# A selective scan behind a deformable convolution: delta*u*B made by ScalarE and TensorE in two one-bank PSUM tiles, one state at a time

## The chip, the cores and the metric

The kernel runs on one core of a Trainium2 chip. Its engines are TensorE (PE, with its weight loads as PEld), VectorE (DVE), ScalarE (ACT), GpSimd (POOL) and SyncE (SP, which issues most DMAs). Each works through its own queue in order, and semaphores hold an instruction until what it needs is there. The metric is the device time of one execution in microseconds; less is better.

## The reference, cut to what matters

Two layers, each `x = x + layer(group_norm(x))`, on x of 4 images x 128 x 128 x 128 channels, float32. The first is a deformable convolution in two groups (offsets, bilinear samples gathered from the image, a depthwise and a pointwise convolution). The second is two Mamba blocks, for which every image row of 128 pixels is a sequence of its own. The change lies in the scan of such a block:

```python
xz = h @ in_w
u, res = jnp.split(xz, 2, axis=-1)
u = silu(causal_conv4(u))                      # 256 channels
dt, Bm, Cm = jnp.split(u @ xw, [8, 24], axis=-1)   # 16 states
delta = softplus(dt @ dtw + dtb)
A = -jnp.exp(A_log)
# per sequence, channel d and state n, over time t:
#   h[t] = exp(delta[t,d] * A[d,n]) * h[t-1] + delta[t,d] * u[t,d] * Bm[t,n]
#   y[t,d] = sum over n of h[t] * Cm[t,n]
y = y + u * Dp
return y * silu(res) @ ow
```

## The kernel before

**First layer.** `layer0(b)` walks image b in 32 x 9 = 288 units. For each unit `gather` issues eight indirect DMAs on GpSimd (line 364), which fetch the bilinear neighbours of 128 pixels each into `gt`. `sample` multiplies them by their weights on VectorE (`gw`, line 382), adds the four neighbours by accumulating transposes on TensorE into one PSUM bank `p4` (in the profile `p`; the helper `add_transposed`, line 128), and ScalarE copies that bank out (`s`, line 396). `add_up` then adds nine taps into the accumulators `acc` (line 415), some 60 matmul instructions for each of five units in nine.

**Second layer.** A job is four image rows (512 time steps, four sequences) of one Mamba block; there are 128 x 2 = 256 jobs. `pre` prepares a job: `u`, `g`, the projection `dbl` that holds dt, B and C, then `delta` (tile `de`) and `du` = delta*u, both with channels on the partitions, in NC = 2 chunks of 128 channels. `pre` of the next job is emitted ahead of `main` of this one. `main` takes the 16 states in eight steps of NQ = 2 states. In each step:

- SP broadcasts two rows of B and two of C over all partitions from DRAM (`bc`, 512 KB each, line 570);
- ScalarE computes the decays exp(delta*A) into one of three tiles `da` that all steps share (line 580); the first element of each sequence is set to zero (line 575), which starts the recurrence anew, so that one scan can run over all of chunks, states and sequences;
- VectorE multiplies du by B into `hs` (line 584), scans `da` in place with `hs` (line 591, 2048 elements a partition) and multiplies by C (line 595);
- TensorE adds the result over states by 16 accumulating transposes into `y` in PSUM, two banks (line 128).

After the last step `g = y * silu(res)` is formed (line 606), transposed back (`pyg`, `yg`) and projected (`pout`).

**Order.** The end of the program emits the units of the next image's first layer among the steps of this image's second layer, so that the first layer of image b+1 ends three jobs before the second layer of image b. The first layer of image 0 runs alone at the start, the second layer of image 3 alone at the end. The order within each engine's queue is then set when the program is built, by a scheduler that follows the emitted order as a priority; nothing is reordered while it runs.

**PSUM.** [...] pool `ps` (first layer, two), `psa` (`acc`, two), `ps1` (preparation and projection, two), `psy` (`y`, two).

Of the kernel before, what the change touches and what calls it, by code (L numbers as in the profile page):

```python
# [10 lines left out]
F32 = mybir.dt.float32  # L11
# [6 lines left out]
P = 128  # L18
# [45 lines left out]
def block_kernel(ctx: ExitStack, tc: tile.TileContext, a: dict, out: bass.AP):  # L64
# [27 lines left out]
    ps = ctx.enter_context(tc.tile_pool(name="l0ps", bufs=2, space=PSUM))  # L92
# [3 lines left out]
    ps1 = ctx.enter_context(tc.tile_pool(name="l1ps", bufs=2, space=PSUM))  # L96
# [29 lines left out]
    def add_transposed(o, v, start, stop):  # L126

        nc.tensor.matmul(o, v, ident, is_transpose=True, start=start, stop=stop, skip_group_check=True)  # L128
# [34 lines left out]
    cvw = loadw("cvw", [P, NL, DCONV, NC * P], pool=p2, tag="hs")  # L163
    for l in range(NL):
        nc.vector.tensor_tensor(
            inc[:, l], cvw[:, l], inw[:, l].unsqueeze(1).to_broadcast([P, DCONV, NC * P]), ALU.mult
        )
# [295 lines left out]
    das = [cw.tile([P, NC, NQ, SR, P], F32, name=f"da{i}") for i in range(NDA)]  # L463
    zero = cw.tile([P, NC * NQ * SR], F32, name="zero")
    nc.vector.memset(zero, 0.0)
# [18 lines left out]
    def pre(st, l):  # L484
# [40 lines left out]
        bcd = pd.tile([2 * NS, TB], F32, tag="bcd", name=f"bcd_{nm}")  # L525
        nc.sync.dma_start(bcd, dbl[DTR + 1 : XP, :])
# [3 lines left out]
        du = p2.tile([P, NC, TB], F32, tag="du", name=f"du_{nm}", bufs=2)  # L530
# [20 lines left out]
        st.update(u=u, g=g, delta=de, du=du, bcd=bcd)  # L551

    def main(st, l):
# [11 lines left out]
        for q in range(NS // NQ):  # L565
            bc = []
            for w in range(2):
                t = p2.tile([P, NQ, TB], F32, tag=f"bc{w}", name=f"bc{w}_{nm}_{q}", bufs=2)
                n0 = w * NS + q * NQ
                nc.sync.dma_start(t, st["bcd"][n0 : n0 + NQ, :].partition_broadcast(P))  # L570
                bc.append(t)
            da = das[n_da[0] % NDA]
            n_da[0] += 1

            nc.scalar.copy(da.rearrange("p c n s t -> p (c n s) t")[:, :, 0], zero)
            for c in range(NC):
                dv = st["delta"][:, c].rearrange("p (s t) -> p s t", s=SR)
                for n in range(NQ):
                    s = q * NQ + n
                    nc.scalar.activation(  # L580
                        da[:, c, n, :, 1:], dv[:, :, 1:], AF.Exp, scale=aneg[:, l, c, s : s + 1]
                    )
            hs = p2.tile([P, NC, NQ, TB], F32, tag="hs", name=f"hs_{nm}_{q}")
            nc.vector.tensor_tensor(  # L584
                hs,
                st["du"].unsqueeze(2).to_broadcast([P, NC, NQ, TB]),
                bc[0].unsqueeze(1).to_broadcast([P, NC, NQ, TB]),
                ALU.mult,
            )
            df = da.rearrange("p c n s t -> p (c n s t)")  # L590
            nc.vector.tensor_tensor_scan(  # L591
                df, df, hs.rearrange("p c n t -> p (c n t)"), 0.0, ALU.mult, ALU.add
            )
            dc = da.rearrange("p c n s t -> p c (n s t)")
            nc.vector.tensor_tensor(  # L595
                dc, dc,
                bc[1].rearrange("p n t -> p (n t)").unsqueeze(1).to_broadcast([P, NC, NQ * TB]),
                ALU.mult,
            )
            for c in range(NC):  # L600
                for n in range(NQ):
                    for i in range(SR):
                        add_transposed(y[:, i, c], da[:, c, n, i, :], False, q == NS // NQ - 1 and n == NQ - 1)
            yield
# [142 lines left out]
```

## Time and profile before

| | |
|---|---|
| Median of 3 runs | 28,022.95 us (27,987.81 to 28,037.46) |
| The profiled execution, its own time | 28,027.08 us |
| Its span, first to last instruction | 28,025.3 us |
| Mean granted TensorE clock | 0.834 |
| PE busy | 19,874.5 us (71%), 112,196 instructions |
| PEld busy | 13,790.6 us (49%) |
| DVE busy | 22,925.4 us (82%), 11,994 instructions |
| ACT busy | 11,640.4 us (42%), 18,190 instructions |
| POOL busy | 18,817.1 us (67%), 9,222 instructions |
| DMA | 3,804 MB, 136 GB/s in the mean |

The profile gives the busy time of each engine over the span and over forty equal slices, then groups of instructions by line: how often, busy time, mean duration of one in ns, and the idle time of the engine just before them with what ended it. L591 is line 591 of the kernel. A tile's buffer number is left out of its name. TensorE's busy time counts overlapping instructions once and says nothing of its speed; the row PEclk gives the clock that it was granted, in tenths of full speed. An average over the whole span mixes three stretches with different work, so the stretches have to be read apart.

### The profile page before, as it was taken

The page shows a single profiled execution, that of the slowest core. Times are in us where ns is not written, and L with a number is a line of the kernel's source. Part 1 is how long each engine was busy: PE and PEld are TensorE (multiplying, and loading weights), DVE is VectorE, ACT ScalarE, POOL GpSimd, SP SyncE. Part 2 cuts the span into 40 slices and gives each one's busy share as a digit, 9 for nine tenths or more (in the row PEclk, how much of TensorE's full clock was granted, in tenths as well). Part 3 has the DMA queues.
Part 4 walks back from the last instruction along what each step waited for, and adds up shares of the span by engine and source line. Part 5 has one row for each costly group of instructions (what it writes and reads, how often), then busy time and mean ns, then how long its engine had stood idle before and what let it go on. Part 6 is the DMA issues. An engine that isn't in the chain of part 4 may idle for free. (4 is left out here: it accounts for less than half of the span.)

```text
span 28025.3 us, 292712 instructions
## 1 busy us (share of the span) xinstructions
PE 19874.5 (71%) x112196; PEld 13790.6 (49%) x112196; DVE 22925.4 (82%) x11994; ACT 11640.4 (42%) x18190; POOL 18817.1 (67%) x9222
## 2 busy tenths in 40 slices
PE   4777777777777777777777777777777755555555
PEld 3444455555555545555555555555555544434344
DVE  2232288888888898888888898888888899999999
ACT  0000144444444444444444444444444455555554
POOL 4777788888888878888888878888888800000000
PEclk7888888888888888888888888888888877667777
DMA  5363344455444444445444444444444433333333
GB/s 142 114 168 107 111 142 145 146 161 162 149 142 139 142 135 146 147 151 168 152 142 144 139 138 140 144 142 144 140 143 143 138 113 107 109 107 109 107 109 104
DMA packets 1994584, 3804.39 MB, mean 136 GB/s; under 512 B 771795, under 2 KB 1116115, under 8 KB 1993052
## 3 DMA queue, kind: packets, MB, share of 16 engines
q1 hardware_dynamic: 1550812, 2577.13, 28.6%
q0 software_dynamic: 442368, 1208.55, 13.6%
q8 instruction: 880, 14.42, 0.2%
q14 instruction: 524, 4.29, 0.0%
HBM read 3567.63 MB, written 217.05 MB: 135 GB/s over the span
## 5 line engine op out<-in xcount | busy, mean ns | idle before, releaser
L364 POOL DMA_INDIRECT gt<-table,idx x9216 | 18816.4, 2042 | 3674.8 <-issue 3042.2
L591 DVE TENSOR_TENSOR_SCAN da<-da,hs 128x2048 f32<-128x2048 f32 x2048 | 9056.4, 4422 | 498.9 <-ACT da L580 407.2
L128 PE MATMUL y<-ident,da 128*128 128x128 f32 x32768 | 5361.3, 331 | 4518.1 <-DVE da L595 4515.5
L580 ACT ACTIVATE da<-de,aneg 128x508 f32<-128x508 f32 x8192 | 5569.7, 713 | 6349.2 <-PE y L128 6151.5
L128 PEld LDWEIGHTS y<-ident,da 128*128 128x128 f32 x32768 | 4780.2, 174 | 5499.1 <-DVE da L595 3050.8
L415 PE MATMUL acc<-s,wc 128*64 128x256 f32 (+3 forms) x38400 | 6435.8, 457 | 887.3 <-ACT s L396 885.9
L382 DVE TENSOR_TENSOR gw<-gt,wt 128x1024 f32<-128x1024 f32 x2304 | 2794.9, 1219 | 3919.9 <-DMA gt<-table,idx 3268.9
L415 PEld LDWEIGHTS acc<-s,wc 128*64 128x64 f32 x38400 | 3399.3, 147 | 3237.7 <-issue 1456.8
L595 DVE TENSOR_TENSOR da<-da,bc 128x2048 f32<-128x2048 f32 x2048 | 4688.0, 2289 | 25.5
L584 DVE TENSOR_TENSOR hs<-du,bc 128x2048 f32<-128x2048 f32 x2048 | 4680.3, 2285 | 0.0
L128 PE MATMUL p<-ident,gw 128*128 128x128 f32 x18432 | 2790.5, 304 | 2015.4 <-DVE gw L382 2007.3
L128 PEld LDWEIGHTS p<-ident,gw 128*128 128x128 f32 x18432 | 2361.0, 158 | 2609.6 <-DVE gw L382 2036.7
L396 ACT COPY s<-p 128x512 f32<-128x512 f32 x1152 | 669.8, 582 | 4377.9 <-PE p L128 4370.7
L501 PE MATMUL pu<-hp,inc 128*128 128x512 f32 x4096 | 1808.3, 593 | 0.0
L580 ACT ACT_TABLE_LOAD x1019 | 1307.4, 1283 | 10.2
L501 PEld LDWEIGHTS pu<-hp,inc 128*128 128x128 f32 x4096 | 751.9, 189 | 865.1 <-issue 864.9
L508 ACT ACTIVATE u<-pu,w_cvb 128x512 f32<-128x512 f32 x512 | 324.0, 683 | 1448.5 <-PE y L561 1442.5
L611 PE MATMUL pyg<-ident,g 128*128 128x128 f32 x2048 | 366.0, 337 | 522.0 <-DVE g L606 521.9
L561 PEld LDWEIGHTS y<-ddiag,u 128*128 128x128 f32 x4096 | 585.1, 202 | 197.6 <-issue 197.6
L546 ACT ACT_TABLE_LOAD x506 | 649.2, 1283 | 9.0
L612 ACT COPY yg<-pyg 128x512 f32<-128x512 f32 x512 | 284.9, 588 | 813.3 <-PE pyg L611 813.2
L561 PE MATMUL y<-ddiag,u 128*128 128x128 f32 x4096 | 614.4, 285 | 0.0
(118 smaller groups left out, 11438.6 us busy)
## 6 DMA issues: line engine op xcount, KB each, us to landing
bc<-bcd SPq DMA_DIRECT2D x4096, 512.0 KB
gt<-table,idx POOLq DMA_INDIRECT x9216
table<-xt SPq DMA_DIRECT2D x984, 128.0 KB
xt<-in_x SPq DMA_DIRECT2D x124, 320.0 KB
xr<-in_x SPq DMA_DIRECT2D x128, 256.0 KB
x<-xo SPq DMA_DIRECT2D x128, 256.0 KB
x1t<-x SPq DMA_DIRECT2D x128, 256.0 KB
x1t_o<-x SPq DMA_DIRECT2D x128, 256.0 KB
```

The lines of the kernel that those rows point to most:

```text
L128: nc.tensor.matmul(o, v, ident, is_transpose=True, start=start, stop=stop, skip_group_check=True)
L364: nc.gpsimd.indirect_dma_start(out=gt[:, v, r], out_offset=None, in_=flat, in_offset=bass.IndirectOffsetOnAxis(ap=idx[:, ri, o : o + 1], a ...
L382: nc.vector.tensor_tensor(gw.rearrange("p r s v c -> p (r s) v c"), gts[h].rearrange("p v r (s c) -> p (r s) v c", c=CG), wv.unsqueeze(3). ...
L396: nc.scalar.copy(st[:, :, 1 : W + 1], p4)
L415: nc.tensor.matmul(accs[b, j + i0][CG * g : CG * g + CG, q : q + rb - ra, :], wc[sl, v, e, :], st[p + 4 * g if p < 4 else 8][sl, ra:rb, kx ...
L501: nc.tensor.matmul(px.rearrange("p (s t) -> p s t", s=SR), inc[:, l, j, c * P : (c + 1) * P], h[:, :, j : j + P], start=(j == 0), stop=(j ...
L546: nc.scalar.activation(du[:, c], w1, AF.Ln)
L561: nc.tensor.matmul(y[:, i, c], st["u"][:, c, i * P : (i + 1) * P], ddiag[:, l, c, :], start=(i % 2 == 0 and c == 0), stop=False, skip_grou ...
L580: nc.scalar.activation(da[:, c, n, :, 1:], dv[:, :, 1:], AF.Exp, scale=aneg[:, l, c, s : s + 1])
L584: nc.vector.tensor_tensor(hs, st["du"].unsqueeze(2).to_broadcast([P, NC, NQ, TB]), bc[0].unsqueeze(1).to_broadcast([P, NC, NQ, TB]), ALU.mult,
L591: nc.vector.tensor_tensor_scan(df, df, hs.rearrange("p c n t -> p (c n t)"), 0.0, ALU.mult, ALU.add)
L595: nc.vector.tensor_tensor(dc, dc, bc[1].rearrange("p n t -> p (n t)").unsqueeze(1).to_broadcast([P, NC, NQ * TB]), ALU.mult,)
```

## The change

delta*u*B is no longer a VectorE product with a broadcast B. With time on the partitions, B[t, n] is one scalar per partition: `pre` transposes B (`bt`) and du (`dut`) once per job, with TensorE and a ScalarE copy. In `main` the loop goes over single states. ScalarE scales `dut` by `bt` into `xs`, four instructions of 128x256; TensorE transposes `xs` back into `px`, one PSUM bank for each chunk of channels, from a pool `psx` of two banks; VectorE scans 512 elements at a time, with the decays from SBUF and the addend straight from `px`, into `hs`. Only C is still broadcast (`cs`). The decay tiles `da` hold one state, are no longer overwritten by the scan, and keep the zeros at the start of sequences for the whole run. The two banks come from `ps` and `ps1`, which have one bank each now; `du` has one buffer. Line numbers of the changed kernel are ten to twenty higher below the changed places.

```diff
-    ps = ctx.enter_context(tc.tile_pool(name="l0ps", bufs=2, space=PSUM))
+    ps = ctx.enter_context(tc.tile_pool(name="l0ps", bufs=1, space=PSUM))
...
-    ps1 = ctx.enter_context(tc.tile_pool(name="l1ps", bufs=2, space=PSUM))
+    ps1 = ctx.enter_context(tc.tile_pool(name="l1ps", bufs=1, space=PSUM))
+    psx = ctx.enter_context(tc.tile_pool(name="l1psx", bufs=2, space=PSUM))
...
-    das = [cw.tile([P, NC, NQ, SR, P], F32, name=f"da{i}") for i in range(NDA)]
-    zero = cw.tile([P, NC * NQ * SR], F32, name="zero")
-    nc.vector.memset(zero, 0.0)
+    das = [cw.tile([P, NC, SR, P], F32, name=f"da{i}") for i in range(NDA)]
+    for t in das:
+        nc.vector.memset(t, 0.0)
...
-        bcd = pd.tile([2 * NS, TB], F32, tag="bcd", name=f"bcd_{nm}")
-        nc.sync.dma_start(bcd, dbl[DTR + 1 : XP, :])
+        cd = pd.tile([NS, TB], F32, tag="cd", name=f"cd_{nm}")
+        nc.sync.dma_start(cd, dbl[DTR + 1 + NS : XP, :])
+
+        pbt = ps1.tile([P, SR, XP], F32, tag="t", name=f"pbt_{nm}")
+        for i in range(SR):
+            nc.tensor.transpose(pbt[:, i, :], dbl[:, i * P : (i + 1) * P], ident[0:XP, 0:XP])
+        bt = p2.tile([P, SR, NS], F32, tag="bt", name=f"bt_{nm}", bufs=2)
+        nc.scalar.copy(bt, pbt[:, :, DTR + 1 : DTR + 1 + NS])
...
+        dut = p2.tile([P, SR, NC * P], F32, tag="dut", name=f"dut_{nm}", bufs=2)
+        for k in range(SR // 2):
+            pt = ps1.tile([P, 2, NC, P], F32, tag="t", name=f"pdu_{nm}_{k}")
+            for i in range(2):
+                for c in range(NC):
+                    o = (2 * k + i) * P
+                    nc.tensor.transpose(pt[:, i, c, :], du[:, c, o : o + P], ident)
+            nc.scalar.copy(dut[:, 2 * k : 2 * k + 2], pt.rearrange("p s c d -> p s (c d)"))
...
-        for q in range(NS // NQ):
-            bc = []
-            for w in range(2):
-                t = p2.tile([P, NQ, TB], F32, tag=f"bc{w}", name=f"bc{w}_{nm}_{q}", bufs=2)
-                n0 = w * NS + q * NQ
-                nc.sync.dma_start(t, st["bcd"][n0 : n0 + NQ, :].partition_broadcast(P))
-                bc.append(t)
+        for n in range(NS):
+            if n % NQ == 0:
+                cs = p2.tile([P, NQ, TB], F32, tag="cs", name=f"cs_{nm}_{n}", bufs=2)
+                nc.sync.dma_start(cs, st["cd"][n : n + NQ, :].partition_broadcast(P))
             da = das[n_da[0] % NDA]
             n_da[0] += 1
-
-            nc.scalar.copy(da.rearrange("p c n s t -> p (c n s) t")[:, :, 0], zero)
             for c in range(NC):
                 dv = st["delta"][:, c].rearrange("p (s t) -> p s t", s=SR)
-                for n in range(NQ):
-                    s = q * NQ + n
-                    nc.scalar.activation(
-                        da[:, c, n, :, 1:], dv[:, :, 1:], AF.Exp, scale=aneg[:, l, c, s : s + 1]
-                    )
-            hs = p2.tile([P, NC, NQ, TB], F32, tag="hs", name=f"hs_{nm}_{q}")
+                nc.scalar.activation(da[:, c, :, 1:], dv[:, :, 1:], AF.Exp, scale=aneg[:, l, c, n : n + 1])
+
+            xs = p2.tile([P, SR, NC * P], F32, tag="xs", name=f"xs_{nm}_{n}", bufs=2)
+            for i in range(SR):
+                nc.scalar.activation(xs[:, i], st["dut"][:, i], AF.Copy, scale=st["bt"][:, i, n : n + 1])
+            hs = p2.tile([P, NC, TB], F32, tag="hs", name=f"hs_{nm}_{n}", bufs=3)
+            for c in range(NC):
+                px = psx.tile([P, SR, P], F32, tag="x", name=f"px_{nm}_{n}_{c}")
+                for i in range(SR):
+                    nc.tensor.transpose(px[:, i, :], xs[:, i, c * P : (c + 1) * P], ident)
+                nc.vector.tensor_tensor_scan(
+                    hs[:, c],
+                    da[:, c].rearrange("p s t -> p (s t)"),
+                    px.rearrange("p s t -> p (s t)"),
+                    0.0, ALU.mult, ALU.add,
+                )
             nc.vector.tensor_tensor(
-                hs,
-                st["du"].unsqueeze(2).to_broadcast([P, NC, NQ, TB]),
-                bc[0].unsqueeze(1).to_broadcast([P, NC, NQ, TB]),
-                ALU.mult,
-            )
...
+                hs, hs, cs[:, n % NQ].unsqueeze(1).to_broadcast([P, NC, TB]), ALU.mult
             )
             for c in range(NC):
-                for n in range(NQ):
-                    for i in range(SR):
-                        add_transposed(y[:, i, c], da[:, c, n, i, :], False, q == NS // NQ - 1 and n == NQ - 1)
-            yield
+                for i in range(SR):
+                    add_transposed(y[:, i, c], hs[:, c, i * P : (i + 1) * P], False, n == NS - 1)
+            if n % NQ == NQ - 1:
+                yield
```

More of the change, by code (lines that the diff above doesn't have):

```diff
@@ L162, in block_kernel @@
     inw = loadw("inw", [P, NL, NC * P], a["inw"][:, :, 0 : NC * P], pool=p2, tag="yg")
-    cvw = loadw("cvw", [P, NL, DCONV, NC * P], pool=p2, tag="hs")
     for l in range(NL):
+        cvw = p2.tile([P, DCONV, NC * P], F32, tag="dut", name=f"w_cvw_{l}", bufs=2)
+        nc.sync.dma_start(cvw, a["cvw"][:, l])
         nc.vector.tensor_tensor(
-            inc[:, l], cvw[:, l], inw[:, l].unsqueeze(1).to_broadcast([P, DCONV, NC * P]), ALU.mult
+            inc[:, l], cvw, inw[:, l].unsqueeze(1).to_broadcast([P, DCONV, NC * P]), ALU.mult
         )
@@ L524, in pre @@
         nc.scalar.activation(dbl, pdb[0:XP], AF.Identity, bias=xpb)
-        bcd = pd.tile([2 * NS, TB], F32, tag="bcd", name=f"bcd_{nm}")
-        nc.sync.dma_start(bcd, dbl[DTR + 1 : XP, :])
+        cd = pd.tile([NS, TB], F32, tag="cd", name=f"cd_{nm}")
[5 more added lines that the diff above has]
+        nc.scalar.copy(bt, pbt[:, :, DTR + 1 : DTR + 1 + NS])
         de = p2.tile([P, NC, TB], F32, tag="de", name=f"de_{nm}", bufs=2)
-        du = p2.tile([P, NC, TB], F32, tag="du", name=f"du_{nm}", bufs=2)
+        du = p2.tile([P, NC, TB], F32, tag="du", name=f"du_{nm}")
         es, pdts = [], []
@@ L550, in pre @@
         nc.vector.tensor_tensor(du, de, u, ALU.mult)
-        st.update(u=u, g=g, delta=de, du=du, bcd=bcd)
+        dut = p2.tile([P, SR, NC * P], F32, tag="dut", name=f"dut_{nm}", bufs=2)
[6 more added lines that the diff above has]
+            nc.scalar.copy(dut[:, 2 * k : 2 * k + 2], pt.rearrange("p s c d -> p s (c d)"))
+        st.update(u=u, g=g, delta=de, dut=dut, bt=bt, cd=cd)
     def main(st, l):
@@ L584, in main @@
-            nc.vector.tensor_tensor(
-                hs,
-                st["du"].unsqueeze(2).to_broadcast([P, NC, NQ, TB]),
-                bc[0].unsqueeze(1).to_broadcast([P, NC, NQ, TB]),
-                ALU.mult,
-            )
[L590 to L598, printed above, removed]
+                nc.scalar.activation(da[:, c, :, 1:], dv[:, :, 1:], AF.Exp, scale=aneg[:, l, c, n : n + 1])
+            xs = p2.tile([P, SR, NC * P], F32, tag="xs", name=f"xs_{nm}_{n}", bufs=2)
+            for i in range(SR):
+                nc.scalar.activation(xs[:, i], st["dut"][:, i], AF.Copy, scale=st["bt"][:, i, n : n + 1])
```

## The prediction

> **What bounds the kernel now.** I read the page's slices first, since the kernel has three stretches with different limits, then busy time by stretch.
>
> ```profile
> DVE  2232288888888898888888898888888899999999
> POOL 4777788888888878888888878888888800000000
> PEclk7888888888888888888888888888888877667777
> ...
> 3475.00:22490.00 19015.00, 14410.70 (x83124) 9994.29 (x83124) 16770.24 (x8740) 8550.84 (x13424) 16383.25 (x6881) 0.87 0.45 145
> 22490.00:28025.00 5535.00, 2921.43 (x13387) 2246.46 (x13385) 5176.03 (x2093) 2830.02 (x4312) 2.50 (x1) 0.71 0.31 108
> ```
>
> The window rows give length, then busy PE, PE loads, DVE, ACT, POOL, clock, DMA share, GB/s. Until 3475 us only the convolution of image 0 runs. Then both layers run: 1509 of 2048 scans, eight per job, so 188.6 jobs at 100.8 us (**mixed**). From 22490 the second layer is alone: 67.4 jobs at 82.1 us (**tail**). Busy us per job, mixed: PE 76, DVE 89, ACT 45, POOL 87; tail: PE 43, DVE 77, ACT 42.
>
> The tail is DVE's. The mixed stretch looks like DVE's as well, but the gathers decide it (groups of 10500 to 16600, then the timeline):
>
> ```profile
> L364 POOL DMA_INDIRECT gt<-table,idx x2207 | 5264.1, 2385 | 839.7 <-issue 647.9 <-DVE gw L382 161.5 <-DVE fl L292 12.1
> ...
> 15000.46 4.42 DVE L591 TENSOR_TENSOR_SCAN da<-da,hs 128x2048 f32<-128x2048 f32 x1
> 15001.49 4.16 POOL L364 DMA_INDIRECT gt<-table,idx  x1 [0.30 <-issue]
> 15004.92 2.29 DVE L595 TENSOR_TENSOR da<-da,bc 128x2048 f32<-128x2048 f32 x1
> ...
> 7394.96 1.23 DVE L606 TENSOR_TENSOR g<-y,g 128x1024 f32<-128x1024 f32 x1 [0.97 <-PE y L128]
> 7395.02 0.22 ACT L575 COPY da<-zero 128x16 f32<-128x16 f32 x1
> 7395.11 0.95 POOL L364 DMA_INDIRECT gt<-table,idx  x1 [0.30 <-issue]
> ```
>
> A gather costs 2.385 us plus 0.30 us of issue; 36.5 a job make 98 of the 100.8 us: **POOL is the pace of the mixed stretch.** Yet the gather itself takes 0.95 us. The one that starts under a scan with two SBUF operands ends 0.77 us after the scan; the one under L606, which reads y from PSUM, is not delayed. From 6000 to 16000 us no gather of 59 that started under L606 or L548 (both with a PSUM operand) took over 0.95 us; 728 under scans averaged 4.35 us.
>
> The tail's groups (23000 to 28000), which carry my prices:
>
> ```profile
> L591 DVE TENSOR_TENSOR_SCAN da<-da,hs 128x2048 f32<-128x2048 f32 x489 | 2163.8, 4425 | 303.2 <-ACT da L580 256.2 <-DVE hs L584 2.4
> L580 ACT ACTIVATE da<-de,aneg 128x508 f32<-128x508 f32 x1952 | 1346.5, 713 | 1454.1 <-PE y L128 1393.3
> L584 DVE TENSOR_TENSOR hs<-du,bc 128x2048 f32<-128x2048 f32 x489 | 1117.3, 2285 | 0.0
> L595 DVE TENSOR_TENSOR da<-da,bc 128x2048 f32<-128x2048 f32 x488 | 1117.0, 2289 | 10.6
> ```
>
> And the two speeds of a transpose, tail and mixed: 0.22 us each in the first line, 0.11 in the second.
>
> ```profile
> 25047.43 3.65 PE L128 MATMUL y<-ident,da 128*128 128x128 f32 x16 [6.58 <-DVE da L595]
> ...
> 15017.78 3.17 PE L128 MATMUL y<-ident,da 128*128 128x128 f32 x27
> ```
>
> [...]
>
> **The change, part by part** (a pair of states = one old step).
>
> *DVE.* Removed: 2.285 (L584) + 4.425 + 2.289 = 9.00 us per pair. Added: four 512-element scans and two 128x1024 products. [...] so 512 give 1.22 us; the PSUM operand adds about nothing (L548 from PSUM 0.684 us, L547 from SBUF 0.674). No row has this scan: 1.15 to 1.35 us are its bounds (4 us a job either way). A 128x1024 product is 1.22 us (L382). Sum 7.34 us: 1.66 less per pair, 13.2 per job. DVE: mixed 89 to **75.7**, tail 77 to **63.5**.
>
> *POOL.* The scans now read one SBUF operand[...]: per job 16 of L606-sized hs products (19.6 us), nine gw (11) and a few others (4), some 35 of 95 us. A gather then averages about 0.64 x 0.95 + 0.36 x 1.45 = 1.13 us, and 36.5 x 1.43 = **52 us** a job: POOL stops being the pace.
>
> *ACT.* Added: eight xs copies per pair. A 512-element e is 0.63 us, the pointer scale makes it 0.71 (L580), 256 elements fewer take off 0.21: 0.50 long, 0.40 from start to start, as L580's 713 ns go at 0.61. That is 25.6 us a job; plus bt and two dut copies 1.5, plus table loads, 2358 in the program instead of 2045: 1.2 x 1.28 = 1.6; minus the zero copies, about 1. ACT: mixed 45 to **73**, tail 42 to **70**. Edges 0.36 and 0.44 for a copy: 5 us a job.
>
> *PE.* Added: 128 xs transposes a job, eight of du, four for bt: 140 x 0.107 warm = 15 us, x 0.155 (mixed mean: 1191 us / 7699) = 22. Mixed 76 becomes 98 at the present clock; with the bursts closer together I expect it warm: 76 x 0.87 + 15 = **81**. Tail 43 becomes 58 to 65.
>
> *Hidden.* Half of the broadcast reads go (one per pair instead of two, 512 KB each), on SP and DMA engines busy 45%: nothing. Constant loads and memsets run once: nothing. L0's PSUM pool goes from two banks to one; in the first stretch a unit has 3150/288 = 10.9 us and its fill (16 x 0.11) and copy (0.6) need 3, but units wait while the offset convolution uses the bank: 0 to 300 us, I take 100.
>
> *Waits that are added.* The old step had three da buffers of 9 us each. Now ACT is ahead by two or three states, 3.7 us each, PE by one (two banks). While ACT does the next job's preparation (u, g, dbl, e, ln: 10 us, and ten table loads, 13 us), seven states need 7 x 2.82 = 20 more: 43 us against 7 x 3.7 + 5 = 31 of DVE. Less a lead of 3 us, DVE lacks 9 us; ACT's waits in its queue for pyg and pu (350 + 288 us over 60 jobs in the old tail, then harmless) cost some 5 more, since xs and da stand behind them. Preparation has one bank, so each step waits for the one before; it ends at about state 9 of 16, and that slack covers it. In the mixed stretch 60 acc matmuls are one burst of 7.97 us, 2.5 per job. In the issue order px of the next state stands behind it; DVE has 3.7 to 5 us of work meanwhile, so a burst outside the preparation costs about 5 us, inside nothing.
>
> *Sum.* Tail: DVE needs 2 x 1.22 + 1.22 and 0.04 of waits, 3.7 us a state, and 6.3 us a job in L547 to L550 and L606: 16 x 3.7 + 6.3 = 65.5; (9 + 5 from the waits) = **80** us a job, 2 less than now. Mixed: 75.7 + 14 + 2.5 x ½ x 5 = 6, + ACT's s copies 3, - 4 of convolution work that falls into the gaps = **95**, 6 less than now. Total 3475 + 100 + 188.6 x 95 + 67.4 x 80 = **26,900 us**, against a profiled 28,027 (span 28,025), 0.01% above the median 28,023.
>
> **Rivals.**
> 1. *Queues too short (slower).* The acc burst and the preparation don't overlap, each burst costs 6 us and the single bank stretches preparation: mixed 106, tail 86: 3575 + 19,990 + 5,800 = **29,400**. For: ACT, DVE and PE all at 70 to 81 us a job with one state of buffer. Against: gathers no longer hold DVE (3269 us of L382's waits today). It decides from mixed 101 us up.
> 2. *TensorE becomes the bound (slower).* At today's clock PE needs 98 us a job and 5 of waits, 103: with the tail at 80, 3575 + 19,430 + 5,390 = **28,400**. [...]
> 3. *Near the busiest engine (faster).* Preparation fits into slack: mixed 84, tail 74: 3575 + 15,840 + 4,990 = **24,400**.
> 4. [...] (the change does not free POOL): gathers under scans then last until the scan's end. Each is 1.22 us, so a gather is at most 1.6 and POOL 69 us: no bound either; mixed 96.
>
> **Numbers.** Forecast with rival 4 0.50, rival 1 0.24, rival 2 0.14, rival 3 0.12. About 0.2% (56 us) is what a measurement can tell from none. The forecast's edges (mixed 90 to 101, tail 76 to 83) are 25,700 to 28,240, so about 0.04 of it lies at no change and 0.02 above. Faster: 0.44 + 0.12 + 0.02 of rival 2's lower edge = 0.58; same 0.05; slower 0.37. The forecast's own range is 25,700 to 28,200; the range reaches into rivals 1 and 3: 25,000 to 29,500.
>
> **What would show it.** Scans near 1.22 us and products 1.22; gathers near 1.1 us with POOL below 60% busy in the mixed stretch [...]; xs copies 0.50 us; PE's clock above 0.9; DVE waiting for PE px in the middle of a job, and PE behind ACT xs. Mixed over 101 us a job makes the forecast wrong, a tail over 86 makes rival 1 right.

## The result and the profile after

The changed kernel takes 28,381.64 us in the median of four runs (28,374.65 to 28,395.24), the kernel before 28,021.02 us, timed beside it on the same chip (27,987.81 to 28,037.46). The ratio is 1.0131 [1.0113, 1.0148]: **slower by 1.3%**, where 4% faster was forecast. The profiled span is 28,379.0 us.

The page's slices come first, as before (tenths of each of forty slices), then two rows of the window view: length, then busy PE, PE loads, DVE, ACT, POOL, clock, DMA share, GB/s.

```profile
PE   4777788989889889888988888988888887777777
DVE  2232367676767777776767776777666777777777
...
POOL 4777744444444334444444424444444410000000
PEclk7888899999999999999999999999999999888988
...
3450.00:22875.00 19425.00, 17375.94 (x109190) 11545.37 (x109189) 13780.29 (x13228) 13765.05 (x24642) 8384.08 (x6866) 0.98 0.32 101
22875.00:28379.00 5504.00, 4207.62 (x23072) 2917.86 (x23072) 4214.31 (x3745) 4721.51 (x8496) 0.00 (x0) 0.89 0.17 58
```

GpSimd fell from eights to fours and VectorE from eights to sevens, as intended. PE took their place at the top, and its clock rose from 0.87 to 0.98. Counting jobs as in the prediction (1505 of 2048 pairs of states in the mixed stretch, so 188.1 jobs, and 67.9 in the tail):

| us per job | mixed, forecast | mixed, measured | tail, forecast | tail, measured |
|---|---|---|---|---|
| length | 95 | 103.3 (before 100.8) | 80 | 81.0 (before 82.1) |
| PE busy | 81 | **92.4** | 58 to 65 | 61.9 |
| DVE busy | 75.7 | 73.3 | 63.5 | 62.0 |
| ACT busy | 73 | 73.2 | 70 | 69.5 |
| POOL, issue counted | 52 | 55.6 (44.6 busy, 36.5 x 0.30 of issue) | | |

The forecast was 3575 + 17,917 + 5392 us for the three stretches; measured were 3450 + 19,425 + 5504. So nearly the whole miss, 1508 us of 1495 net, lies in the mixed stretch, and there the one busy time that is off is TensorE's.

The costliest groups of the page (busy us and mean ns of one; then idle time just before, and what ended most of it):

```profile
L366 POOL DMA_INDIRECT gt<-table,idx x9216 | 10790.8, 1171 | 12073.3 <-DVE gw L384 9165.9
L600 DVE TENSOR_TENSOR_SCAN hs<-da,px 128x512 f32<-128x512 f32 x8192 | 9610.8, 1207 | 5207.2 <-PE px L599 5129.9
...
L594 ACT ACTIVATE xs<-dut,bt 128x256 f32<-128x256 f32 x16384 | 7139.1, 497 | 1470.5 <-PE px L599 1421.0
...
L606 DVE TENSOR_TENSOR hs<-hs,cs 128x1024 f32<-128x1024 f32 x4096 | 4991.6, 1219 | 58.9
```

The sizes are those of the prediction: scan 1.207 us (forecast 1.22), product 1.219 (1.22), xs copy 0.497 (0.50), gather 1.171 (1.13). Two of these forecasts can be had as estimates from rows of the kernel before. Its products of 1024 and 2048 elements took 1.219 and 2.285 us (L382, L584), which leaves 2 x 1.219 - 2.285 = 0.153 fixed; with the same for a scan, 512 elements need (4.425 - 0.153) / 4 + 0.153 = 1.22. ScalarE's `xo` of 128 and of 384 elements took 0.365 and 0.573 (L343, L351), so 256 elements make 0.21, and L580's 0.71 less 0.21 is 0.50. What is new stands in the second half of the lines: GpSimd idles until VectorE's `gw` frees a `gt` buffer, and VectorE idles until TensorE's `px` comes. The waits of 10500 to 16600 us (59 jobs; total, times, longest) say the same by stage:

```profile
POOL gt L366 <- DVE gw L384: 2814.5, 237, 88.6
DVE hs L600 <- PE px L599: 1181.8, 250, 24.5
```

That is 20 us a job in which VectorE stands still for `px`. The timeline of one such stretch (start, busy us, engine, line):

```profile
12004.20 0.66 PE L599 MATMUL px<-ident,xs 128*128 128x128 f32 x4 [0.39 <-DVE hs L600]
...
12006.32 2.32 DVE L600 TENSOR_TENSOR_SCAN hs<-da,px 128x512 f32<-128x512 f32 x2
...
12007.52 0.95 POOL L366 DMA_INDIRECT gt<-table,idx  x1 [0.30 <-issue]
...
12009.68 1.22 DVE L606 TENSOR_TENSOR hs<-hs,cs 128x1024 f32<-128x1024 f32 x1
...
12011.97 5.38 PE L417 MATMUL acc<-s,wc 64*64 64x384 f32 x36
...
12017.78 1.04 PE L599 MATMUL px<-ident,xs 128*128 128x128 f32 x8
12019.01 2.31 DVE L600 TENSOR_TENSOR_SCAN hs<-da,px 128x512 f32<-128x512 f32 x2
```

Three things are in it. The four transposes of a bank come only after a scan has released that bank (first line). A gather under a scan is not delayed (0.95 us). And the scans pause from 12008.64 to 12019.01; the longest thing that TensorE does meanwhile is a burst of 36 `acc` matmuls, which stands ahead of the next `px`. Which of these costs what, the trace alone doesn't say.

### The profile page after: what moved, and what is told of

The parts are those of the page before. It is cut to its first block, busy times and chain, and to the rows that moved or that the text cites. A ratio compares the mean times of both kernels' runs of the same rounds, so it can differ in the third digit from the quotient of the medians.

```text
span 28379.0 us, 385627 instructions
## 1 busy us (share of the span) xinstructions
PE 24053.6 (85%) x148036; PEld 16090.0 (57%) x148036; DVE 18984.2 (67%) x18140; ACT 18759.3 (66%) x33607; POOL 10791.5 (38%) x9222
## 4 chain that ended last, share of the span: by engine, by line
DVE 28%; PE 28%; issue 19%; POOL 11%; ACT 9%; DMA 3%; SPq 1%; DVEq 0%; POOLq 0%; ACTq 0%
DVE hs L600 17%; POOL gt L366 11%; DVE hs L606 8%; PE acc L417 7%; PE y L129 5%; PE pu L503 4%; PE px L599 3%; DMA gt<-table,idx 2%; ACT xs L594 2%; DVE gw L384 2%; ACT da L590 2%; PE pof L265 1%; ACT L590 1%; PE pdt L542 1%; ACT L554 1%
## 5 line engine op out<-in xcount | busy, mean ns | idle before, releaser
L366 POOL DMA_INDIRECT gt<-table,idx x9216 | 10790.8, 1171 | 12073.3 <-DVE gw L384 9165.9
L600 DVE TENSOR_TENSOR_SCAN hs<-da,px 128x512 f32<-128x512 f32 x8192 | 9610.8, 1207 | 5207.2 <-PE px L599 5129.9
L594 ACT ACTIVATE xs<-dut,bt 128x256 f32<-128x256 f32 x16384 | 7139.1, 497 | 1470.5 <-PE px L599 1421.0
L599 PE MATMUL px<-ident,xs 128*128 128x128 f32 x32768 | 5562.1, 292 | 2046.4 <-DVE hs L600 1445.9
L599 PEld LDWEIGHTS px<-ident,xs 128*128 128x128 f32 x32768 | 3779.3, 146 | 4035.0 <-DVE hs L600 1986.1
L129 PE MATMUL y<-ident,hs 128*128 128x128 f32 x32768 | 4729.9, 288 | 819.5 <-DVE hs L606 795.6
L606 DVE TENSOR_TENSOR hs<-hs,cs 128x1024 f32<-128x1024 f32 x4096 | 4991.6, 1219 | 58.9
L129 PEld LDWEIGHTS y<-ident,hs 128*128 128x128 f32 x32768 | 3771.9, 146 | 2180.6 <-DVE hs L606 1623.6
L129 PEld LDWEIGHTS p<-ident,gw 128*128 128x128 f32 x18432 | 2195.2, 147 | 1268.3 <-issue 517.4
L555 DVE SCALAR_TENSOR_TENSOR e<-w,e 128x512 f32<-128x512 f32 x512 | 350.0, 684 | 471.5 <-ACT w L553 471.2
```

The lines of the kernel that those rows point to most:

```text
L366: nc.gpsimd.indirect_dma_start(out=gt[:, v, r], out_offset=None, in_=flat, in_offset=bass.IndirectOffsetOnAxis(ap=idx[:, ri, o : o + 1], a ...
L594: nc.scalar.activation(xs[:, i], st["dut"][:, i], AF.Copy, scale=st["bt"][:, i, n : n + 1])
L599: nc.tensor.transpose(px[:, i, :], xs[:, i, c * P : (c + 1) * P], ident)
L600: nc.vector.tensor_tensor_scan(hs[:, c], da[:, c].rearrange("p s t -> p (s t)"), px.rearrange("p s t -> p (s t)"), 0.0, ALU.mult, ALU.add,)
L606: nc.vector.tensor_tensor(hs, hs, cs[:, n % NQ].unsqueeze(1).to_broadcast([P, NC, TB]), ALU.mult)
```

## The experiments

**The theories.** The expectations below set four accounts of the lost time against each other. Q: `px` stands in TensorE's queue behind first-layer matmuls, and VectorE waits for it. A: ScalarE's 28 us more a job set the pace. B: the two lost PSUM banks do. W (from e6 on): TensorE has too much work, wherever `px` stands. A fifth is that the freed GpSimd was worth little to begin with. None came out whole: the runs leave TensorE's work (W) with somewhat over half of px's cost, and its exchange of banks with VectorE with the rest.

All ratios are to the kernel before, timed beside the run on the same chip. On the two chips of e1 to e4 and of e5, e6 and e9 the first stretch took 4190 to 4340 us instead of some 3450, so that the us per job are compared as well. The kernel before took 28,619 us on the one and 28,828 on the other; by an estimate from these two, a difference between kernels of both chips is uncertain by some 1 us a job.

### One part of the change at a time: e1, e2, e3

Each keeps all of the change but one part of delta*u*B, whose values are replaced by constants. In e1 neither `xs` nor `px` is made:

```diff
-            for i in range(SR):
-                nc.scalar.activation(xs[:, i], st["dut"][:, i], AF.Copy, ...)
...
-                px = psx.tile(...)
-                for i in range(SR):
-                    nc.tensor.transpose(px[:, i, :], xs[:, i, ...], ident)
+                px = pxs[c]          # two PSUM banks filled once, before the jobs
```

e2 keeps the `xs` copies (nobody reads them); e3 keeps the transposes but reads a constant SBUF tile, `inc`, in place of `xs`.

> The changed kernel with the addend of every scan a constant: px is written once per chunk at the start, and neither the xs copies on ACT nor the px transposes on PE are made per state (bt and dut are still made). What is left is the short scan that reads PSUM. Theory Q (PE's queue: px of the next state stands behind first-layer matmuls and DVE waits 20 us a job for it) and rival A (ACT's 28 us more a job set the pace) both expect DVE's work with short waits: mixed stretch 84 to 90 us a job, tail 68 to 73, together 24,000 to 25,300 us. Rival B (the two lost banks set the pace: preparation and the units of the first layer wait for their single bank) expects the mixed stretch to stay above 97, together above 26,500.

> The changed kernel with constant px as in the run before, but with the xs copies on ACT still made for every state (nobody reads them). Theory Q expects ACT's 73 us a job to hide beside DVE: mixed 86 to 92, tail 72 to 77, together 24,700 to 26,000 us. Rival A expects nearly all of the lost time back: mixed 98 to 103, tail 79 to 82, together 27,300 to 28,400.

> The changed kernel with the px transposes made for every state, but from a constant tile in SBUF, so that ACT makes no xs copies. Theory Q expects the mixed stretch to stay near 97 to 102 us a job, the tail at 72 to 78, together 26,500 to 28,000 us. Rival A expects mixed 85 to 90, tail 70 to 74, together 24,200 to 25,500.

Measured: e1 24,671 us, ratio 0.8628 [0.8614, 0.8643]; e2 26,045, 0.9105 [0.909, 0.912]; e3 28,993, 1.0131 [1.0114, 1.0148]. Window rows, mixed stretch and tail of e1, of e2 and of e3:

```profile
4200.34:20263.36 16063.02, 13819.23 (x85191) 9242.19 (x85192) 13689.56 (x13245) 9624.45 (x13090) 8838.37 (x6871) 0.95 0.40 122
20263.36:24666.60 4403.24, 3276.42 (x14316) 2302.11 (x14314) 4077.41 (x3729) 3211.56 (x4274) 0.00 (x0) 0.71 0.22 71
```

```profile
4192.52:20688.22 16495.70, 13968.94 (x85195) 9305.98 (x85196) 13718.01 (x13248) 14270.16 (x25154) 8769.92 (x6871) 0.94 0.39 119
20688.22:26043.40 5355.18, 3429.23 (x14312) 2357.70 (x14310) 4198.27 (x3726) 4763.53 (x8508) 0.00 (x0) 0.67 0.18 59
```

```profile
4237.57:24146.89 19909.32, 17354.48 (x109197) 11602.72 (x109198) 13786.68 (x13229) 9260.02 (x12702) 8193.07 (x6871) 0.97 0.32 99
24146.89:28975.30 4828.41, 3921.60 (x23071) 2754.90 (x23068) 4079.59 (x3745) 3227.34 (x4285) 0.00 (x0) 0.95 0.20 66
```

Divided by the jobs of each stretch (188.0 to 188.5 and 67.5 to 67.9):

| us a job | mixed | tail |
|---|---|---|
| e1, neither | 85.3 | 65.1 |
| e2, `xs` alone | 87.5 (+2.2) | 79.3 (+14.2) |
| e3, `px` alone | 105.9 (+20.6) | 71.1 (+6.0) |
| the change, both | 103.3 | 81.0 |

Two stretches, two answers. In the **tail** ScalarE is what costs, 14.2 us, as much as the 14 us that the forecast gave its preparation. In e2's tail the scans wait for ScalarE's decays, 907 us from 21500 to 26000 us, in some nine short waits a job:

```profile
DVE hs L605 <- ACT da L597: 907.3, 492, 4.3
```

That fits the forecast's account, a lead that the preparation uses up, but no run took the preparation away. In the **mixed** stretch ScalarE costs 2.2 us and `px` all the rest; A falls there. All three tails lie off what Q expected, and e3's mixed stretch lies over every range. It is even 2.6 us longer than that of the change, which makes the copies as well; why is open. The PE columns size the term that failed: e1 has 73.4 us a job of other work, e3 92.3, so 128 transposes add 18.9 us of busy time, **0.148 us each**, not 0.107.

### Is it TensorE's own work, or its exchange with VectorE? e9

The transposes are made as in e3, but into one bank that nobody reads; the scans read another, constant bank. The addend is constant, as in e3.

```diff
-    psx = ctx.enter_context(tc.tile_pool(name="l1psx", bufs=2, space=PSUM))
+    psx = ctx.enter_context(tc.tile_pool(name="l1psx", bufs=1, space=PSUM))
+    psc = ctx.enter_context(tc.tile_pool(name="l1psc", bufs=1, space=PSUM))
...
-                    nc.tensor.transpose(px[:, i, :], xs[:, i, c * P : (c + 1) * P], ident)
+                    nc.tensor.transpose(px[:, i, :], inc[:, 0, i, c * P : (c + 1) * P], ident)
...
-                    px.rearrange("p s t -> p (s t)"),
+                    pxc.rearrange("p s t -> p (s t)"),
```

> The changed kernel with all px transposes made, from a constant tile and into one bank that nobody reads, and with no xs copies; the scans read one constant PSUM bank for both chunks. TensorE has the same instructions as with px from a constant, but VectorE waits for none of them and they wait for no scan. Theory Q expects mixed 87 to 93 us a job, little over the 85 with no px at all; rival W expects 99 to 106, as with px that is read. Tail: 65 to 70 by both.

Measured: 26,472 us, 0.9182 [0.9167, 0.9197]. The mixed stretch of e9 in the window view:

```profile
4335.90:22266.74 17930.84, 16128.32 (x105715) 11349.08 (x105716) 13811.27 (x13246) 9698.53 (x13096) 8628.04 (x6871) 0.97 0.36 110
```

It is 95.2 us a job, and the tail takes 62.2. But this row has 3482 matmuls fewer than e3's. Nothing holds the transposes back in e9, and 3578 of the 32,768 had run before the mixed stretch began; only 109 a job fell into it instead of 128. From 8000 us on it is 128 a job again. So e1, e9 and e3 are compared from 8000 to 20000 us (141.2, 123.8 and 114.2 jobs by their scans), in this order; the last row has e9's `px` instructions alone.

```profile
8000.00:20000.00 12000.00, 10318.10 (x63563) 6896.14 (x63562) 10218.60 (x9869) 7206.79 (x9802) 6556.64 (x5113) 0.95 0.39 120
8000.00:20000.00 12000.00, 10802.98 (x71384) 7695.50 (x71384) 9055.59 (x8660) 6386.26 (x8603) 5525.34 (x4447) 0.97 0.35 106
8000.00:20000.00 12000.00, 10462.64 (x65761) 6998.01 (x65760) 8333.51 (x7986) 5624.65 (x7710) 4867.73 (x4090) 0.97 0.32 98
...
8000.00:20000.00 12000.00, 2663.83 (x15836) 1829.12 (x15836) 0.97 0.35 106
```

A job takes 85.0, 97.0 and 105.1 us there, with PE busy 73.1, 87.3 and 91.6. So 12.0 us come from TensorE's work alone, with no one waiting for its result, and 8.1 from the exchange: the wait for a free bank and the wait for a filled one. The result lies between the ranges of Q and W; each has a part. Ungated, the transposes add (87.3 - 73.1) / 128 = 0.111 us each, about the forecast's 0.107; gated by scans, 0.145. The rows of the changed kernel's timeline show where the difference comes from: four transposes alone are busy for 0.66 us, eight in a row for 1.04. Four more cost some 0.4 us, and the rest, over 0.2, comes once for every burst. In e3 and the changed kernel as in e9 a transpose starts 0.109 us after the one before it, in the median. So gating does not make a transpose slower; it leaves more bursts standing alone, each with its end, and PE's 92 us of busy time hold some 4 us of such ends (an estimate, (0.145 - 0.111) x 128), which belong to the exchange.

### Take work off TensorE elsewhere: e7 in both kernels

Three of the nine taps are added in `add_up`, so that TensorE has 13.5 us a job less to do; the other six taps of the convolution are left out. All other engines do what they did.

```diff
-        for e in range(NT):
+        for e in (0, 4, 8):
```

> The changed kernel with three of the nine taps of the first layer's sums, so that TensorE has some 13 us a job less to do in the mixed stretch (60 matmuls of 7.97 us become 20). If TensorE's load makes px late, mixed falls by 8 to 14 us a job, to 89 to 95. If it is the exchange between engines whatever the load, by 0 to 4 us, to 99 to 103. Tail unchanged at 81.

> The kernel before with the same three taps. GpSimd is its pace in the mixed stretch, so nothing but the first stretch can get shorter: mixed 98 to 101 us a job (100.8 with nine taps), tail 82. If TensorE counted here as well, mixed would fall below 96.

Measured: the change 26,004 us, 0.9239 [0.9224, 0.9255]; the kernel before 28,218, 1.0026 [1.0016, 1.0036]. Mixed stretches of the change and of the kernel before, each with three taps:

```profile
3452.56:20512.88 17060.32, 14839.73 (x90104) 10185.20 (x90103) 13777.97 (x13234) 13820.65 (x24761) 8434.22 (x6864) 0.96 0.37 115
```

```profile
3435.73:22678.84 19243.11, 12753.40 (x63861) 8998.12 (x63860) 16706.40 (x8725) 8582.44 (x13385) 16624.76 (x6877) 0.79 0.45 143
```

In the changed kernel PE falls from 92.4 to 78.9 us a job and the stretch from 103.3 to 90.7: **12.6 us gained for 13.5 us of TensorE's work**. The same cut in the kernel before gains nothing (102.2 against 100.8; POOL is busy 88.3). So the pace of the mixed stretch passed from GpSimd to TensorE. The kernels set side by side (mixed, us a job; e9 from 8000 to 20000 us; e10 is described below):

| | PE busy | DVE busy | clock | length | length less PE |
|---|---|---|---|---|---|
| e1 | 73.4 | 72.7 | 0.95 | 85.3 | 11.9 |
| e7, changed kernel | 78.9 | 73.2 | 0.96 | 90.7 | 11.8 |
| e9 | 87.3 | 73.2 | 0.97 | 97.0 | 9.7 |
| the change | 92.4 | 73.3 | 0.98 | 103.3 | 10.9 |
| e3 | 92.3 | 73.3 | 0.97 | 105.9 | 13.6 |
| e10 | 93.1 | 73.8 | 0.99 | 101.3 | 8.2 |

VectorE's work is the same in all of them. The length follows TensorE's, and lies 8 to 14 us above it. e1 has such a gap too, 11.9 us, though nothing waits for `px` there; what makes it up was not tested.

### The bursts and the order of the queue: e10, e6, e12

e10 breaks the `acc` burst into three parts of three taps, emitted among the steps of the second layer:

```diff
-    def add_up(b, j, p, st):
+    def add_up(b, j, p, st, taps):
...
-        for e in range(NT):
+        for e in taps:
...
-            if u >= 4:
-                add_up(b, j, u - 4 if u < 8 else 4, st)
+            for k in range(3):
+                if u >= 4:
+                    add_up(b, j, u - 4 if u < 8 else 4, st, range(3 * k, 3 * k + 3))
+                if k < 2:
+                    yield
...
-    n0 = NJ * NT
+    n0 = 3 * NJ * NT
```

> The changed kernel with the same instructions, but the first layer's sums of a unit are emitted in three parts of three taps among the steps of the scan, so that the scheduler puts fewer long bursts of them before px (127 places with twenty or more of them between two px instructions instead of 390). If half of px's 20 us a job is waiting behind these bursts, it saves 3 to 7 us a job: mixed 96 to 100, ratio to the kernel before 0.97 to 0.995. If TensorE's work alone holds px up, wherever the bursts are, mixed stays at 102 to 105 and the ratio at 1.00 to 1.02.

Measured: 28,024 us, 1.0004 [0.9995, 1.0013]; mixed 101.3, tail 81.1. Its wait for `px` (10500 to 16600 us):

```profile
DVE hs L603 <- PE px L602: 1096.3, 295, 25.9
```

Bursts in thirds save 2 us a job, less than the 3 to 7 expected here; VectorE still waits 18 us a job for `px` (20 in the changed kernel), and the longest wait is no shorter. How much whole bursts cost, a cut in three doesn't tell. It is a cheap repair, back to the time of the kernel before and no further.

e6 puts the whole body of a state ahead of everything else in the scheduler's order:

```diff
+            with tc.high_priority(offset=3000):
                 da = das[n_da[0] % NDA]
...
```

> The changed kernel with the same instructions in another order: everything that one state of the scan needs (decays, xs, px, scan, product with C, sum over states) is put ahead of the first layer's work for the scheduler, so that px stands behind fewer first-layer matmuls: 185 places with ten or more of them between two px instructions, where the changed kernel has 493. Theory Q (the order of PE's queue makes DVE wait 20 us a job) expects these waits to be cut by half or more, mixed 92 to 98 us a job, ratio to the kernel before 0.94 to 0.98. Rival W (TensorE has too much work: 92 us busy of 103 leave no room, wherever px stands) expects mixed 100 to 106 and a ratio of 1.00 to 1.03.

Measured: 32,298 us, 1.1198 [1.1179, 1.1217]; mixed 115.7, tail 92.7. Its waits of 10500 to 16600 us:

```profile
DVE e L556 <- ACT w L554: 680.8, 85, 24.5
...
DVE gw L385 <- PE p L130: 455.6, 143, 21.0
...
DVE hs L602 <- PE px L601: 392.9, 214, 21.5
```

The wait for `px` fell to about a third (393 us from 1182), as Q expected, and the total got worse, outside both ranges, since the preparation and the convolution are now late in its place: in the changed kernel `e` waited 154 us for `w` and `gw` 39 us for `p`, here 681 and 456. PE busy rose to 97.6 us. Here, taking one wait away by order alone moved it to other chains in the same full queue.

e12 gives `px` a third bank, which the two one-bank pools pay for by sharing theirs:

```diff
-    ps1 = ctx.enter_context(tc.tile_pool(name="l1ps", bufs=1, space=PSUM))
-    psx = ctx.enter_context(tc.tile_pool(name="l1psx", bufs=2, space=PSUM))
+    ps1 = ps
+    psx = ctx.enter_context(tc.tile_pool(name="l1psx", bufs=3, space=PSUM))
```

> The changed kernel with three PSUM banks for px instead of two; the third comes from letting the first layer and the preparation share one bank. If the exchange of two banks between PE and VectorE (px waits until a scan has read its bank, and holds up what stands behind it) is what is left of px's cost, VectorE's waits for px fall by a third or more: tail 75 to 79 us a job (81 with two banks), mixed 97 to 101 unless the shared bank eats it, ratio to the kernel before 0.96 to 1.00. If it is the order of PE's queue and TensorE's work, the tail stays at 80 to 82 and mixed at 102 or above, ratio 1.01 to 1.05.

Measured: 29,537 us, 1.0545 [1.0528, 1.0563]; mixed 109.5, tail 80.9. Its wait for `px` (10500 to 16600 us):

```profile
DVE hs L600 <- PE px L599: 1167.6, 337, 12.0
```

The tail, where no first layer wants the shared bank, is not moved by a third bank (81.0 with two). The mixed stretch lost 6 us, outside both ranges, and VectorE waits 21 us a job for `px`, no less than with two banks. The convolution's wait for its bank grew (in the same window ScalarE's `s` waited for `p` 510 us instead of 133), and the clock was 0.90. So the price of the sharing may hide what a third bank brings, and the depth of `px` stays open in the mixed stretch.

### The lost banks by themselves: e4

The kernel before, with one bank in `l0ps` and in `l1ps`:

```diff
-    ps = ctx.enter_context(tc.tile_pool(name="l0ps", bufs=2, space=PSUM))
+    ps = ctx.enter_context(tc.tile_pool(name="l0ps", bufs=1, space=PSUM))
...
-    ps1 = ctx.enter_context(tc.tile_pool(name="l1ps", bufs=2, space=PSUM))
+    ps1 = ctx.enter_context(tc.tile_pool(name="l1ps", bufs=1, space=PSUM))
```

> The kernel before with nothing changed but the two PSUM pools of the first layer and of the preparation, which get one bank each instead of two. Theory Q expects GpSimd to stay the pace of the mixed stretch and DVE that of the tail, so 28,000 to 28,250 us. Rival B expects at least the loss that the change shows, 28,400 us or more.

```profile
4201.10:22939.59 18738.49, 14404.64 (x82989) 9837.95 (x82988) 16751.11 (x8728) 9357.03 (x13990) 16192.47 (x6868) 0.87 0.47 147
```

Measured: 28,277 us, 0.9887 [0.9871, 0.9904]; mixed 99.4 (row above), tail 77.9, beside a kernel before of 28,619 us. Two banks fewer made the kernel before *faster*, by 1.1%. By themselves the banks cost nothing there, and e1, which has the same single banks as the change, needs only 85.3 us a job; B falls. Whether they cost something beside the full queue of the change wasn't tried. Why they help the kernel before is open.

### What undelayed gathers are worth without TensorE: e5, e8, e11

e5 is the kernel before, but VectorE writes its product du*B to two PSUM banks and scans 1024 elements from there. TensorE and ScalarE get no new work.

```diff
-            hs = p2.tile([P, NC, NQ, TB], F32, tag="hs", ...)
-            nc.vector.tensor_tensor(hs, ...)                       # 2048
-            nc.vector.tensor_tensor_scan(df, df, hs, ...)          # 2048, hs in SBUF
+            for n in range(NQ):
+                hs = psx.tile([P, NC, TB], F32, tag="x", ...)      # PSUM
+                nc.vector.tensor_tensor(hs, st["du"], bc[0][:, n] ..., ALU.mult)
+                df = da[:, n].rearrange("p c s t -> p (c s t)")
+                nc.vector.tensor_tensor_scan(df, df, hs ..., 0.0, ALU.mult, ALU.add)
```

> The kernel before with one thing of the change alone: scans whose addend lies in PSUM. delta*u*B stays a VectorE product with the broadcast B, one state at a time, but is written to two PSUM banks (taken, as in the change, from the first layer's and the preparation's pools), and the scan goes over 1024 elements; ScalarE and TensorE do nothing new. If the operand in PSUM is what frees GpSimd, gathers take 0.95 us under scans, some 1.5 us in the mean, POOL is no longer the pace and DVE is, with 91 us of work a job: mixed 92 to 97 us a job, tail 77 to 82, ratio to the kernel before 0.94 to 0.97. If the short scans of the change free it by their length, gathers stay at 1.8 us or more and the ratio at 0.98 to 1.02.

Measured: 27,560 us, **0.9558 [0.9543, 0.9574]**; mixed 94.3, tail 81.5. The mixed stretch of e5, two groups of its page, and a piece of its timeline:

```profile
4270.64:22020.56 17749.92, 14259.20 (x82927) 9470.99 (x82927) 17068.52 (x11732) 9495.34 (x14093) 9888.42 (x6869) 0.90 0.49 155
...
L365 POOL DMA_INDIRECT gt<-table,idx x9216 | 12319.0, 1337 | 9690.3 <-DVE gw L383 6558.3
...
L590 DVE TENSOR_TENSOR_SCAN da<-da,hs 128x1024 f32<-128x1024 f32 x4096 | 9352.7, 2283 | 248.3 <-DVE hs L586 6.1
...
12002.17 2.28 DVE L590 TENSOR_TENSOR_SCAN da<-da,hs 128x1024 f32<-128x1024 f32 x1
12003.40 0.95 POOL L365 DMA_INDIRECT gt<-table,idx  x1 [0.31 <-issue]
12004.36 1.20 DVE L383 TENSOR_TENSOR gw<-gt,wt 128x1024 f32<-128x1024 f32 x1
12004.65 1.73 POOL L365 DMA_INDIRECT gt<-table,idx  x1 [0.30 <-issue]
```

The gather inside the scan takes 0.95 us, the one that starts in the product `gw` with its two SBUF operands 1.73. All 920 gathers that started under a scan between 8000 and 14000 us took no more than 0.96. The product that feeds the scan (L586) still reads two SBUF operands, and the 444 gathers that started under it took 1.43 us in the mean, though it writes to PSUM. POOL falls from 87 to 52.5 us a job, and VectorE, at 90.7 of 94.3, is the pace. Against e4, which has one bank in the same two pools, moving one operand to PSUM brings 5.1 us a job in the mixed stretch and costs 3.6 in the tail, where there are no gathers: two scans of 2.283 us for one of 4.425 and two products of 1.227 for one of 2.285 are 8 x 0.31 = 2.5 us of that. The rival "little worth" falls: undelayed gathers were worth having, and they could be had with no new work on TensorE.

e8 goes half way: chunk 0 is made by ScalarE and TensorE, chunk 1 by VectorE's product, into the two banks of one tile that a single scan of 1024 elements reads.

```diff
-            xs = p2.tile([P, SR, NC * P], ...)
+                xs = p2.tile([P, SR, P], ...)
...
+                    nc.tensor.transpose(hs[:, 0, i * P : (i + 1) * P], xs[:, i], ident)
+                nc.vector.tensor_tensor(hs[:, 1], st["du"][:, 1], bc[0][:, n], ALU.mult)
...
+                    df, df, hs.rearrange("p c t -> p (c t)"), 0.0, ALU.mult, ALU.add
```

> A mix: chunk 0 of delta*u*B goes the way of the change (xs on ScalarE, px on TensorE), chunk 1 is a VectorE product into the second PSUM bank, and one scan of 1024 elements goes over both. VectorE has 83 us of work a job in the mixed stretch and 71 in the tail, TensorE some 68 transposes a job more than before. If px costs in proportion to TensorE's free time (24 us a job before), half of them fit: mixed 88 to 93, tail 73 to 78, ratio 0.91 to 0.94. If each px costs the same 0.16 us as in the change, 10 us come on top of VectorE's waits: mixed 94 to 99, ratio 0.95 to 0.98.

Measured: 28,287 us, 1.0099 [1.0082, 1.0116]; mixed 99.7 with PE 84.5 and DVE 82.6, tail 89.6, both over what was expected. One of its waits, 10500 to 16600 us:

```profile
DVE hs L603 <- PE hs L602: 857.8, 378, 16.6
```

L603 is the VectorE product, and it waits for TensorE's transposes into the other half of the same tile: that tile has no second buffer, so both chunks and the scan take turns. As a test of "half the load" it is spoilt by that wait, and what a middle way with two tiles would bring stays open.

e11 takes e5 for the first 189 jobs and, from there on, where no gathers are left, the product and the 2048-element scan of the kernel before from SBUF:

```diff
+            if st["late"]:                      # job >= 189
+                hs = p2.tile([P, NQ, NC, TB], F32, tag="hs", ...)
+                nc.vector.tensor_tensor(hs, ...)                   # 2048
+                nc.vector.tensor_tensor_scan(df, df, hs ..., 0.0, ALU.mult, ALU.add)
+            else:
                 for n in range(NQ):
```

> The kernel with VectorE products into PSUM, and in the tail (from job 189 of 256, where no gather runs) the step of the kernel before, one scan of 2048 elements from SBUF with one bank for preparation. Mixed 94 us a job as with products into PSUM everywhere, tail 78 as in the kernel before with one bank: ratio 0.945 to 0.951. If the tail does not care for the length of the scans, 0.954 to 0.958.

Measured: 26,475 us, **0.9458 [0.9442, 0.9474]**; it beats both kernels. Slices, scan groups and windows of e11:

```profile
DVE  2232289999999999999999999999999999999999
...
POOL 3777755555555535555555545556555500000000
...
L604 DVE TENSOR_TENSOR_SCAN da<-da,hs 128x1024 f32<-128x1024 f32 x3024 | 6901.2, 2282 | 148.1 <-ACT da L582 4.5
...
L594 DVE TENSOR_TENSOR_SCAN da<-da,hl 128x2048 f32<-128x2048 f32 x536 | 2370.1, 4422 | 48.0 <-ACT da L582 7.9
...
3445.40:21168.96 17723.56, 14230.72 (x82927) 9460.74 (x82927) 17066.62 (x11732) 9490.57 (x14093) 9818.22 (x6872) 0.91 0.49 156
21168.96:26457.70 5288.74, 3085.51 (x13517) 2294.03 (x13514) 5197.98 (x2121) 3171.46 (x4620) 0.00 (x0) 0.72 0.34 114
```

VectorE is at nine tenths throughout, and the scans wait for almost nothing (148 and 48 us in the whole run): 94.2 us a job in the mixed stretch with 90.7 of VectorE's work, 77.9 in the tail with 76.6. What is left is nearly all VectorE's own work.

### The changed kernel once more

> The changed kernel once more, beside the next three on one chip: ratio to the kernel before 1.00 to 1.02, mixed stretch 103 us a job, tail 81.

28,378 us, 1.0133 [1.0116, 1.015], with 103.3 and 80.9 us a job: the difference stands.

## Why the prediction was wrong

**The failed step is the PE term, and that it was then counted as hidden.** The prediction wrote "76 x 0.87 + 15 = 81" and left TensorE out of the sum "75.7 + 14 + 6 + 3 - 4 = 95". Measured were 92.4 of 103.3. The term has two halves, and both were too small:

- *The old work at the full clock* ("warm" in the forecast), 66 us. The factor 0.87 assumed full speed, and busy time in proportion to the clock. The clock did rise, to 0.98 (0.95 in e1). But e1 has 73.4 us a job, of which the twelve new transposes of the preparation take 1.9; so the old work fell from 76.4 to about 71.5, 5 us and not 10. In proportion to e1's clock it would have been 6 to 7. In the traces of both kernels the clock was granted at 1.0 or at 0.5, and transposes in a row started 0.109 us apart at the one and 0.213 at the other; the share of 0.5 fell from 27% of the mixed stretch before to 4% after. What keeps the clock up was not shown, and busy time followed the mean clock only in part.
- *The new transposes*, 15 us. The rate of 0.107 us was about right for a run that waits for nothing: at the full clock transposes of the kernel before started 0.109 us apart, and e9 gives 0.111. In bursts of four, each behind the release of a bank by a scan, they added 0.145 to 0.148, that is 18.9 us instead of 13.7.

Nor was the term used. Even at 81 us TensorE would have been the fullest engine of the mixed stretch, ahead of VectorE's 75.7, and the sum was still built on VectorE. The kernels of the table, e1 without any `px` among them, end 8 to 14 us above TensorE's busy time: at 81 that gives 89 to 95, at 92.4 it gives 100 to 106, with 103.3 measured. So it is the size of the term that moved the result.

**The 14 us of waits** were right for the tail (14.2, e1 to e2), where ScalarE is the fullest engine, and wrong for the mixed stretch, where the same copies cost 2.2, with no `px` there to hide them. The tail's 80 us came out at 81.0, with ACT at 69.5 for 70 and DVE at 62.0 for 63.5.

**Bursts.** Six us were forecast; cutting the bursts in three wins back 2 (e10). The timeline shows a burst ahead of the scans' `px`, and yet cutting it up wins back little; the matmuls remain, on the engine that sets the pace.

**The gathers** were read rightly. The scan with a PSUM operand doesn't delay a gather: all 731 gathers that started under a scan between 8000 and 14000 us took at most 0.96 us in the changed kernel, those under the product L606 1.71 in the mean. The gathers came to 1.171 us for 1.13, for which only products with two SBUF operands were taken to delay them. Rival 4, by which scans from PSUM delay gathers all the same, is excluded. That POOL stops being the pace was right, and e5 shows what that alone brings.

**VectorE's savings** (13.2 us a job) were real, 73.3 busy for 75.7, and turned into idle time in front of `px`, 20 us a job.

**The single bank** was to cost 100 us; the first stretch took 3450 us instead of 3475, and in e4 fewer banks rather helped.

**Which rival.** Rival 2, TensorE as the bound, is what happened, with its numbers (103 us a job; 28,400 in all), but not for its reason. It rested on today's clock; what the forecast set against it, a higher clock, was an estimate of the author's that came true (0.98) and didn't save the case. It had 98 of work and 5 of waits where 92.4 and 10.9 were measured; that its sum came out at 103 is luck. Of the signs named beforehand, a PE clock above 0.9, POOL under 60% and VectorE waiting for `px` in mid-job all came, and "mixed over 101 makes the forecast wrong" decided. Rival 1's tail of 86 didn't come.

**Still open:** how the 8 us of exchange divide between the order of the queue and the release of banks (bursts in thirds save 2; e6 and e12 changed more than they were to), what fills the 12 us between TensorE's work and the length in e1, why e3 is longer than the change, and why single banks make the kernel before faster.

## What to carry to other kernels

When work moves to an engine off the critical path, write that engine's new total beside those of the others and ask whether it is now the fullest: here 73 us plus 19 made the new pace, and the stretch ended some 11 us above that sum. Price the moved instructions in the bursts in which they will run (0.145 us a transpose here), not at the rate of an unbroken run (0.111). And look for the cheapest form of the effect that matters: what the mixed stretch needed was one scan operand in PSUM, which VectorE could write there itself (e5 and e11).

## What the runs showed of the hardware

- Gathers that started under a scan with one operand in PSUM took 0.95 us, none of 731 in the changed kernel and of 920 in e5 over 0.96, against 4.35 us in the mean under the scans of the kernel before, 2048 elements with both operands in SBUF. A result in PSUM was not enough: under e5's product of two SBUF operands, which writes to PSUM, 444 gathers took 1.43 us in the mean.
- Scans with the addend in PSUM took 1.207 us for 512 elements (the changed kernel) and 2.283 for 1024 (e5), that is 2.10 ns for each further element. Carried on to 2048 this gives an estimate of 4.435; with both operands in SBUF a scan of 2048 took 4.422.
- A 128x128 float32 transpose added 0.111 us of busy time ungated (e9) and 0.145 in bursts that waited for a bank (e3), at a granted clock of 0.97 in both; a burst of four was busy 0.66 us and one of eight 1.04.
- TensorE's granted clock was recorded as 1.0 or as 0.5 in both kernels. In the kernel before, transposes in a row started 0.109 us apart (median) at 1.0 and 0.213 at 0.5. The clock was at 0.5 for 27% of its mixed stretch and 59% of its tail, in the changed kernel for 4% and 21%.
- PE's old work fell by 6% (76.4 to about 71.5 us a job, the twelve added transposes taken off) while its clock, a mean over the stretch, rose by 9% (0.87 to 0.95, e1).
- Engines followed the order in which the program was built: in the trace of the kernel before, all 11,994 instructions of VectorE, 16,145 of ScalarE (its table loads not counted) and 9,222 of GpSimd come in that order.
